# A two-layer graph attention kernel on one core: the order in which the score products take their operands, for every group of three half-blocks

## The chip, the core and the metric

The kernel runs on one core of a Trainium2 chip. The metric is the device time of one launch in microseconds (us), as the median of several runs; lower is better. TensorE (PE, with its weight loads shown as PEld), VectorE (DVE), ScalarE (ACT) and GpSimd (POOL) compute; SyncE (SP) issues most of the transfers. All data are fp32.

## What is computed

There are 128 graphs of 64 nodes with 768 features. The input is normalised, goes through two attention layers that share one adjacency matrix, and the result is added to the input. Cut to what matters:

```python
h = maximum(layernorm(x), 0)                      # x: 128 x 64 x 768
for l in range(2):
    m_left, m_right = h @ W_left[l].T, h @ W_right[l].T
    u_left  = einsum('bih,bjh->bij', h, m_left) / sqrt(768)
    u_right = einsum('bih,bjh->bij', h, m_right) / sqrt(768)
    u = u_left on and above the diagonal, u_right below it, where adj is set
    attention = exp(u) * adj, each row divided by its sum
    h = relu(layer_norm(attention @ (h @ W_lin[l].T)))
out = x + h
```

## The kernel before

Each layer has two passes. Pass one forms m_left and m_right for all tokens, multiplies them with h to scores, and turns these into attention weights that go to DRAM. Pass two forms h @ W_lin, applies the attention and normalises. The change touches pass one alone.

Pass one works on half-blocks of 256 tokens, called parts in what follows. There are 32: the first two form superblock 0, the other thirty form superblocks 1 to 10 of three parts each (`SUPER`, indexed by k). In a superblock, the multiplication by the two weight matrices, of 3 x 3 blocks each, is done by a fast scheme: `PRODUCTS` lists 40 products of a sum of weight blocks with a sum of token blocks, and `READS` says for each product to which of 18 outputs its running sum is added and with what factor. Output o belongs to part o // 6, to the left (0) or right (1) matrix by o // 3 % 2, and to the third o % 3 of the features; a third is two chunks of 128 features. So outputs 0 to 5 are part 0, 6 to 11 part 1, 12 to 17 part 2. The outputs of a part stand in one tile: in the listings of layer 0 `m_288` is part 0, `m_289` part 1 and `m_290` part 2.

The 40 products run one behind the other on PE, four matmuls of 128x256 each (two records each in the trace, so x8). They are spread over four running sums in four of six PSUM banks (C, D, X, Y, Z, V); product i goes on in the bank of i % 4, and the next superblock begins with the two other banks. `reads(i)` takes product i out of its bank: the first read into an output is a scaled copy on ACT (line 950), each later one an addition on DVE (lines 245 and 954). The next product in the same bank has to wait for that read.

An output is final with its last read. Product 39, the last of a superblock, is read into six outputs: 0, 4, 5 (part 0), 6, 7 (part 1) and 13 (part 2). All other outputs are final earlier.

The scores of superblock k - 1 are computed by `scores(k - 1)` while superblock k is already under way, behind the first four of its products (`SCORED = 3`), and before those four are read:

```python
if i == SCORED and k:
    scores(k - 1)
if i >= SCORED or k == 0:
    for n in waiting:
        reads(n)
```

So four products, some 7 us of PE, lie between the last product of a superblock and its scores. `scores` goes through 6 pairs of graphs q (two for each part) and 6 chunks c, and for each of these 36 units emits four matmuls of 32x95 (line 762, two records each: 288 for a superblock of three parts) that read the tile m of part q // 2 at chunk c and the part's tokens `ht`, and add up in the PSUM tile `sc`. The reads behind the scores overwrite m, so they wait for the units that read the same piece of m.

PE's order is that of the code, and so is DVE's and ACT's: the kernel writes it out by hand, with small jobs hung on numbered slots between the matmuls (`put`, `run`). Two orders exist. For the last superblock of each layer (`k == last`), the six reads of product 39 are sorted by `LAST_READ = (13, 6, 7, 0, 4, 5)` and the units of the scores by `SCORES_LAST`, a list of (part, chunks); for all other superblocks of three parts, reads go by output number and units by part, then pair, then chunk. There a pair's six chunks are one accumulation group of their own (`new` is set for its first chunk), and for the first and the last superblock one group spans all pairs in a bank.

Of the kernel before, what the change touches and what calls it, by code (L numbers as in the profile page):

```python
# [17 lines left out]
def kernel(  # L18
# [16 lines left out]
    C = H // P  # L35
# [31 lines left out]
    def put(slot, *fs):  # L67
        plan.setdefault(slot, []).extend(fs)

    def put_all(slot, fs, step=1):  # L70
        for f in fs:
            if f is not None:
                put(slot, f)
            slot += step
        return slot
# [5 lines left out]
    def run(slot):  # L81
# [30 lines left out]
    PRODUCTS = (  # L112
# [64 lines left out]
    def begins(k, l=0):  # L177
        return 0 if k == 0 else 2 * (len(PRODUCTS) if l else PLAIN) + 2 * len(PRODUCTS) * (k - 1)
# [65 lines left out]
    def added(eng, o, sign, a, b):  # L244
        (eng.tensor_add if sign == "+" else eng.tensor_sub)(o, a, b)  # L245
# [428 lines left out]
    def pass_one(l, start, final):  # L674
        with tc.tile_pool(name=f"one{l}", bufs=2, reuse_waits="tile") as sp, \
# [12 lines left out]
            def load_adj(k, queue=nc.sync):  # L688
                ADJ[k] = sp.tile([P, 6, 2, S], F32, name="adj", bufs=1)
                for u in sorted({p // 2 for p in SUPER[k]}):  # L690
                    at = [i for i, p in enumerate(SUPER[k]) if p // 2 == u]
                    q = [2 * (SUPER[k][i] % 2) for i in at]
                    for h in range(PAIR):
                        queue.dma_start(
                            ADJ[k][h * S:(h + 1) * S, 2 * at[0]:2 * at[-1] + 2].rearrange("p s k i -> p s (k i)"),
                            adj_t[u, h][:, q[0]:q[-1] + 2])
# [13 lines left out]
            def product(bank, w, ts, new, slot, n=TH):  # L710
                p = bank[:, :2 * n].rearrange("p (g n) -> p g n", g=2)
                for g in range(2):
                    for c in range(K2):
                        at = 0
                        for t in ts:
                            t = t[:, c]
                            n = math.prod(t.shape[1:])
                            o = p[:, g, at:at + n]
                            if len(t.shape) == 3:
                                o = o.rearrange("p (b s) -> p b s", b=t.shape[1])  # L720
                            nc.tensor.matmul(o, w[:, c, g * P:(g + 1) * P], t,  # L721
                                             start=(new and g == c == at == 0), stop=(c == K2 - 1),
                                             skip_group_check=True)
                            at += n
                    if g == 0:
                        turn_of(slot)

            def out_of(bank, thirds=False, o=0):
                if thirds:
                    p = bank[:, :4 * CUT].rearrange("p (g b s) -> p g b s", g=2, s=WIDE)  # L730
                    return p[:, :, :, THIRDS[o // 6][1]:]
                return bank.rearrange("p (g b s) -> p g b s", g=2, s=S)

            def into(o, thirds=False):
                v, k, i = o // 6, o // 3 % 2, o % 3
                if thirds:
                    r, n = THIRDS[v]
                    return both[:, i * K2:(i + 1) * K2, :, k, r + n:r + WIDE]
                return M[v][:, i * K2:(i + 1) * K2, :, k, :]

            def scores(k):
                nq = 2 * len(SUPER[k])
                p = KEEP["scores"].rearrange("p a (q m) -> p (a q) m", m=P)
                todo, begun, left = [(q, c) for q in range(nq) for c in range(C)], set(), {}
                if k == last:
                    todo.sort(key=lambda qc: next(n for n, (v, cs) in enumerate(SCORES_LAST)
                                                  if qc[0] // 2 == v and qc[1] in cs))
                if k == 0:

                    todo.sort(key=lambda qc: qc[1] < 3 if l else -(qc[0] // 2))  # L750
                for q, c in todo:
                    ht, m = HT[1, l, SUPER[k][q // 2]], M[q // 2]
                    left[q] = left.get(q, C) - 1
                    for h in range(PAIR):
                        b = q % 2 * PAIR + h
                        mb = both[:, c, q // 2 * PB + b] if l and k == 0 else m[:, c, b]
                        mb = mb.rearrange("p k j -> p (k j)")
                        for e in (0, 32):

                            new = (q // 4, h, e) not in begun if k in (0, last) else left[q] == C - 1  # L760
                            begun.add((q // 4, h, e))
                            nc.tensor.matmul(p[h * S + e:h * S + e + 32, q, e:e + 95],  # L762
                                             ht[:, c, b * S + e:b * S + e + 32], mb[:, e:e + 95],
                                             start=new, stop=not left[q], skip_group_check=k in (0, last))

            def chain(k):
                adj, nq = ADJ[k], 2 * len(SUPER[k])
# [42 lines left out]
            def softmax(k):  # L810
                CHAIN[k] = chain(k)
                return [lambda: next(CHAIN[k], None)] * 8
# [38 lines left out]
            def bank_of(n):  # L851
                n %= BANKS
                return KEEP["CD"][n] if n < 2 else KEEP["XYZV"[n - 2]]
# [79 lines left out]
            last = len(SUPER) - 1  # L933
            for k in range(FIRST_OF[l], len(SUPER)):
                assert slot == begins(k, l)
                if k:
                    put_all(slot + 2 * SCORED + 4, softmax(k - 1), 3)
                    put(slot + 2 * SCORED + 42, lambda k=k: load_adj(k, nc.sync if k == last else nc.scalar))
                if k == last:
                    final(slot, tokens)  # L940
                seen, waiting = set(), []

                def reads(i):
                    at_end = k == last and i == len(PRODUCTS) - 1
                    for o, c in sorted(READS[i], key=lambda oc: LAST_READ.index(oc[0])) if at_end else READS[i]:
                        bank = out_of(bank_of(CHAINS * (k - 1) + i % CHAINS), k == 0, o)
                        to = into(o, k == 0)
                        if o not in seen:
                            seen.add(o)
                            nc.scalar.activation(to, bank, AF.Copy, scale=float(c))  # L950
                        elif abs(c) == 1:
                            added(nc.vector, to, "+" if c > 0 else "-", to, bank)
                        else:
                            nc.vector.scalar_tensor_tensor(to, bank, float(c), to, op0=ALU.mult, op1=ALU.add)  # L954

                for i, (f, t) in enumerate(PRODUCTS):
                    while l and f not in weights.at:
                        fetch.popleft()()
                    w, tok = weights.need(f), tokens.need(k, t)
                    product(bank_of(CHAINS * (k - 1) + i % CHAINS), w, tok, i < CHAINS, slot, TH if k else 2 * CUT)  # L960
                    tokens.used(k, t)
                    if k == last:
                        weights.used(f)
                    waiting.append(i)
# [5 lines that stand above are left out]
                        waiting = []  # L970
                    turn_of(slot + 1)
                    slot += 2
# [5 lines left out]
            for i in (0, 1):  # L978
                LEAD[i] = fresh(l, i, (0, 1))
                multiply(l, 0, i, LEAD[i], (0, 1))  # L980
            scores(last)
            for f in steps[1:4]:
                f()
# [421 lines left out]
```

## Time and profile before

| | |
|---|---|
| runs | 2625.58, 2625.85, 2631.21 us |
| median | 2625.85 us |
| profiled execution | 2632.4 us, of which the span of the program is 2630.5 us |
| granted TensorE clock | 0.997 |
| busy share of the span | PE 98%, PEld 84%, DVE 67%, ACT 36%, POOL 67% |
| DMA | 331.83 MB, mean 126 GB/s |
| score matmuls (line 762) | 6144 records, 138.7 us busy on PE |

The profile is of one execution. Its 1.9 us beside the span are before the first and behind the last instruction. A row of the timeline gives the start and the length in us, the engine, the line, the operation, out<-in, how many instructions were merged into it, and in brackets the engine's idle time just before it with what ended that. Ends of matmuls are modelled, so the starts of the rows on PE are the safer reading. "issue" as the end of an idle time means that the engine waited for nothing that the profile shows.

### The profile page before, as it was taken

The numbers are of one execution on the slowest core, as the hardware profiler recorded it, in microseconds if no ns is written. First come the engines' busy times: TensorE is split into PE (matmuls) and PEld (weight loads), VectorE is DVE, ScalarE is ACT, GpSimd is POOL, SyncE is SP. The second block draws the span as 40 slices with busy tenths as digits, with TensorE's granted clock in tenths as the row PEclk, the third lists the DMA queues.
The fourth block names the chain that finished last, engine by engine and source line by source line (L and its number), as shares of the span: only waits on it lengthen the run. The fifth ranks groups of instructions, "written<-read, shape, count | busy, mean of one in ns | idle before, by whom it ended". The sixth has DMA issues, their size and how long they took to land.

```text
span 2630.5 us, 47267 instructions
## 1 busy us (share of the span) xinstructions
PE 2587.5 (98%) x18122; PEld 2214.9 (84%) x18122; DVE 1773.1 (67%) x2896; ACT 939.1 (36%) x1979; POOL 1756.7 (67%) x1384
## 2 busy tenths in 40 slices
PE   9899999999999999999999999999999999999998
PEld 8788888888888888888788888888888888788886
DVE  7878787777767445554457667677676666666667
ACT  5531213223113244444542222122222345555453
POOL 4766676666668657776267666667666668778776
PEclk9999999999999999999999999999999999999999
DMA  7534435333422354545795434253532215556555
GB/s 221 126 99 105 107 93 127 92 105 79 96 56 63 124 158 149 160 136 177 217 290 124 106 89 104 63 122 94 142 94 70 66 52 160 161 162 172 172 165 144
DMA packets 258464, 331.83 MB, mean 126 GB/s; under 512 B 56002, under 2 KB 190402, under 8 KB 258242
## 3 DMA queue, kind: packets, MB, share of 16 engines
q1 hardware_dynamic: 243106, 321.35, 44.1%
q10 hardware_dynamic: 15136, 7.48, 1.0%
q8 instruction: 145, 2.38, 0.4%
q14 instruction: 77, 0.63, 0.1%
HBM read 213.39 MB, written 115.34 MB: 125 GB/s over the span
## 4 chain that ended last, share of the span: by engine, by line
PE 89%; DVE 5%; ACT 3%; issue 1%; DMA 1%; SPq 0%; POOL 0%; DVEq 0%; ACTq 0%; POOLq 0%
PE Z L1047 13%; PE Y L721 9%; PE X L721 9%; PE C L721 9%; PE D L721 8%; PE Y L1047 8%; PE Z L721 8%; PE V L721 8%; PE X L1047 6%; PE sc L762 5%; PE V L1047 4%; PE aux L1089 2%; DVE m L245 2%; DVE st L352 1%; PE aux L1112 1%
## 5 line engine op out<-in xcount | busy, mean ns | idle before, releaser
L245 POOL TENSOR_TENSOR g<-ht 128x512 f32<-128x512 f32 (+1 forms) x608 | 777.5, 1290 | 404.0 <-ACT ht L395 84.0
L245 POOL TENSOR_TENSOR g<-g,g 128x512 f32<-128x512 f32 (+1 forms) x314 | 400.9, 1285 | 138.1 <-PE C L721 22.6
L245 POOL TENSOR_TENSOR g<-ht,g 128x512 f32<-128x512 f32 (+1 forms) x272 | 346.2, 1282 | 169.8 <-PE Z L721 44.6
L721 PE MATMUL X<-g,g 128*128 128x256 f32 (+1 forms) x1080 | 252.3, 376 | 0.4 <-DVE m L954 0.4
L1047 PE MATMUL Z<-g,g 128*128 128x256 f32 x1024 | 244.2, 380 | 1.1 <-ACT hl L316 0.8
L721 PE MATMUL C<-g,g 128*128 128x256 f32 x1008 | 239.3, 380 | 2.9 <-POOL g L245 2.9
L721 PE MATMUL Y<-g,g 128*128 128x256 f32 (+1 forms) x968 | 226.4, 377 | 7.5 <-POOL g L245 5.6
L721 PEld LDWEIGHTS X<-g,g 128*128 128x128 f32 x1080 | 202.5, 191 | 29.1 <-DVE m L954 1.1
L1047 PEld LDWEIGHTS Z<-g,g 128*128 128x128 f32 x1024 | 191.7, 190 | 33.2 <-issue 2.8
L395 ACT ACTIVATE ht<-ht,b_col,a_col 128x256 f32<-128x256 f32 x384 | 196.3, 592 | 58.9 <-DMA ht<-h 32.1
L721 PE MATMUL Z<-g,g 128*128 128x256 f32 (+1 forms) x936 | 217.0, 375 | 0.0
L721 PEld LDWEIGHTS C<-g,g 128*128 128x128 f32 x1008 | 190.4, 190 | 30.9 <-POOL g L245 4.1
L721 PE MATMUL D<-g,g 128*128 128x256 f32 x880 | 209.6, 381 | 2.3 <-POOL g L245 2.3
L721 PEld LDWEIGHTS Y<-g,g 128*128 128x128 f32 x968 | 182.2, 191 | 32.5 <-POOL g L245 8.9
L721 PE MATMUL V<-g,g 128*128 128x256 f32 (+1 forms) x840 | 193.7, 373 | 1.6 <-issue 1.6
L721 PEld LDWEIGHTS Z<-g,g 128*128 128x128 f32 x936 | 174.5, 190 | 23.0
L721 PEld LDWEIGHTS D<-g,g 128*128 128x128 f32 x880 | 168.2, 191 | 25.7 <-POOL g L245 2.7
L1047 PE MATMUL X<-g,g 128*128 128x256 f32 x768 | 182.5, 379 | 0.0
L721 PEld LDWEIGHTS V<-g,g 128*128 128x128 f32 x840 | 157.0, 190 | 21.6 <-issue 1.8
L1247 POOL TENSOR_TENSOR z<-z,b 128x768 f32<-128x768 f32 x62 | 112.7, 1830 | 82.0 <-DVE z L1244 77.5
L245 DVE TENSOR_TENSOR m<-m,Y 128x512 f32<-128x512 f32 (+2 forms) x196 | 126.4, 667 | 58.9 <-ACT m L950 35.3
L245 DVE TENSOR_TENSOR m<-m,D 128x512 f32<-128x512 f32 x180 | 118.2, 676 | 69.4 <-ACT m L950 51.4
(226 smaller groups left out, 4603.8 us busy)
## 6 DMA issues: line engine op xcount, KB each, us to landing
ht<-h SPq DMA_DIRECT2D x126, 768.0 KB, 6.0
h<-xb SPq DMA_DIRECT2D x124, 384.0 KB, 6.2
z<-z SPq DMA_DIRECT2D x128, 192.0 KB, 3.1
x<-z SPq DMA_DIRECT2D x128, 192.0 KB, 4.3
xr<-in_x_dram SPq DMA_DIRECT2D x120, 192.0 KB, 3.8
out_dram<-xr SPq DMA_DIRECT2D x120, 192.0 KB, 2.7
x<-in_x_dram SPq DMA_DIRECT2D x112, 192.0 KB, 4.7
g<-form SPq DMA_DIRECT2D x40, 256.0 KB, 4.9
```

Source lines behind the costliest of these rows:

```text
L245: (eng.tensor_add if sign == "+" else eng.tensor_sub)(o, a, b)
L352: nc.vector.bn_stats(st[:, n, :], halves[n])
L395: nc.scalar.activation(ht, ht, AF.Relu, bias=cols[1][:, c:c + 1], scale=cols[0][:, c:c + 1])
L721: nc.tensor.matmul(o, w[:, c, g * P:(g + 1) * P], t, start=(new and g == c == at == 0), stop=(c == K2 - 1), skip_group_check=True)
L762: nc.tensor.matmul(p[h * S + e:h * S + e + 32, q, e:e + 95], ht[:, c, b * S + e:b * S + e + 32], mb[:, e:e + 95], start=new, stop=not left ...
L1047: nc.tensor.matmul(p[:, n], b[t][:, c, r * P:(r + 1) * P], w[s][:, c, :], start=(i in FIRST and i not in PRELOAD and n == c == 0), stop=(c ...
L1089: nc.tensor.matmul(cx[k][i, m, :HH], at[j, q, :], hl[j, q, m * HH:(m + 1) * HH], start=True, stop=True)
L1112: nc.tensor.matmul(parts[r, k][n][i], at[j, q, :], hl[j, q, cut], start=True, stop=True)
L1247: nc.gpsimd.tensor_add(zs[k], zs[k], rows["b"])
```

## The change

The order that the last superblock had is given to every superblock but the first of each layer. The reads of product 39 now go 13, 6, 7, 0, 4, 5, and the score units go part 2 at chunks 0, 1, 4, 5; part 1 at chunks 4, 5; part 2 at chunks 2, 3; part 1 at chunks 0 to 3; part 0 at all chunks. The accumulation group spans all pairs of a bank everywhere. It concerns nine superblocks of each layer, 18 in all; the first and the last of each layer stay as they were.

```diff
                 todo, begun, left = [(q, c) for q in range(nq) for c in range(C)], set(), {}
-                if k == last:
+                if k:
                     todo.sort(key=lambda qc: next(n for n, (v, cs) in enumerate(SCORES_LAST)
                                                   if qc[0] // 2 == v and qc[1] in cs))
...
-                            new = (q // 4, h, e) not in begun if k in (0, last) else left[q] == C - 1
+                            new = (q // 4, h, e) not in begun
...
-                                             start=new, stop=not left[q], skip_group_check=k in (0, last))
+                                             start=new, stop=not left[q], skip_group_check=True)
...
-                    at_end = k == last and i == len(PRODUCTS) - 1
+                    at_end = k and i == len(PRODUCTS) - 1
```

The number of instructions stays the same on every engine, and on ACT, POOL and SP their order too. Two places change, both once in each of the 18 superblocks. The first is PE at the scores of superblock 2 in layer 0, between the products in banks Z and V and those in X and Y:

```order
 L721 MATMUL Z<-g_121,g_153 128x256 x4
 L721 MATMUL V<-g_152,g_142 128x256 x4
+L762 MATMUL sc<-m_290,ht 32x95 x32
+L762 MATMUL sc<-m_289,ht 32x95 x16
+L762 MATMUL sc<-m_290,ht 32x95 x16
+L762 MATMUL sc<-m_289,ht 32x95 x32
 L762 MATMUL sc<-m_288,ht 32x95 x48
-L762 MATMUL sc<-m_289,ht 32x95 x48
-L762 MATMUL sc<-m_290,ht 32x95 x48
 L721 MATMUL X<-g_129,g_150 128x256 x4
```

The 144 matmuls of part 0, 1 and 2 have become those of part 2, 1, 2, 1 and 0: part 0 has moved from the front to the end, and part 1 still ends after 96 of 144.

The second is DVE at the reads of product 39 (bank D) of the same superblock:

```order
 L422 SCALAR_TENSOR_TENSOR nb_1850<-mv_1847,rs_1849 128x4
+L245 TENSOR_TENSOR m_290<-m_290,D 128x8x64
+L245 TENSOR_TENSOR m_289<-m_289,D 128x8x64
+L954 SCALAR_TENSOR_TENSOR m_289<-D,m_289 128x8x64
 L245 TENSOR_TENSOR m_288<-m_288,D 128x8x64 x3
-L245 TENSOR_TENSOR m_289<-m_289,D 128x8x64
-L954 SCALAR_TENSOR_TENSOR m_289<-D,m_289 128x8x64
-L245 TENSOR_TENSOR m_290<-m_290,D 128x8x64
 L245 TENSOR_TENSOR m_289<-m_289,Y 128x8x64
```

The same six additions stand there; the three into part 0 have moved behind those into parts 2 and 1.

## The prediction

> **What bounds the kernel now.** I read the page first, for the engine that sets the time.
>
> ```profile
> span 2630.5 us, 47267 instructions
> PE 2587.5 (98%) x18122; PEld 2214.9 (84%) x18122; DVE 1773.1 (67%) x2896; ACT 939.1 (36%) x1979; POOL 1756.7 (67%) x1384
> PE 89%; DVE 5%; ACT 3%; issue 1%; DMA 1%; SPq 0%; POOL 0%; DVEq 0%; ACTq 0%; POOLq 0%
> ```
>
> PE is busy for 98% and holds 89% of the chain of waits, so a change that adds no work can win only PE's idle time. DVE's 5% of the chain is where to look. Next, the groups by line on PE for the score matmuls, and the view of that source line, which counts PE and PEld together.
>
> ```profile
> L762 PE MATMUL sc<-m,ht 128*32 128x95 f32 x6144 | 138.7, 246 | 9.7 <-issue 7.7 <-DVE m L245 1.2
> its engine sat idle before it (us, times) until:
>   issue: 26.2, 54
>   DVE m L245: 6.2, 16
> ```
>
> Line 762 waits for two things: DVE's additions into m, and "issue". The timeline of PE tells them apart. Here are an undisturbed superblock in the old order, one that waits for DVE, and the last superblock of layer 0, which has the new order already.
>
> ```profile
> 165.28 1.89 PE L721 MATMUL D<-g,g 128*128 128x256 f32 x8
> 167.10 4.60 PE L762 MATMUL sc<-m,ht 128*32 128x95 f32 x211
> 172.07 1.92 PE L762 MATMUL sc<-m,ht 128*32 128x95 f32 x77 [0.38 <-issue]
> 173.92 1.99 PE L721 MATMUL Z<-g,g 128*128 128x256 f32 x8
> ...
> 241.36 1.89 PE L721 MATMUL V<-g,g 128*128 128x256 f32 x8
> 243.55 7.04 PE L762 MATMUL sc<-m,ht 128*32 128x95 f32 x288 [0.30 <-DVE m L245]
> 250.52 1.99 PE L721 MATMUL X<-g,g 128*128 128x256 f32 x8
> ...
> 858.44 6.22 PE L762 MATMUL sc<-m,ht 128*32 128x95 f32 x288
> 864.59 1.78 PE L1047 MATMUL Z<-g,g 128*128 128x256 f32 x7
> ```
>
> Without a stop, 288 records take 864.59 - 858.44 = 6.15 us, 21.4 ns each. An "issue" gap comes in the middle of a batch (after record 211 here); a DVE wait comes at its start. The weight loads show that the second kind is three waits.
>
> ```profile
> 243.55 0.32 PEld L762 LDWEIGHTS sc<-m,ht 128*32 128x32 f32 x16 [0.70 <-DVE m L245]
> 244.14 0.32 PEld L762 LDWEIGHTS sc<-m,ht 128*32 128x32 f32 x16 [0.28 <-DVE m L245]
> 244.74 4.06 PEld L762 LDWEIGHTS sc<-m,ht 128*32 128x32 f32 x197 [0.28 <-DVE m L245]
> 249.09 1.28 PEld L762 LDWEIGHTS sc<-m,ht 128*32 128x32 f32 x59 [0.29 <-issue]
> ```
>
> Each 16 records are two chunks: PE stops for chunks 0, 2 and 4 of part 0, that is for outputs 0, 4 and 5, which DVE is just adding. One such batch has 0.30 on PE and 0.70 + 0.28 + 0.28 on PEld, 1.56 in all and four times. The 6.2 us and 16 times of the line are therefore four batches and nothing else, and so are PE's 1.2 us. The other 14 superblocks that the change touches wait for no addition. DVE's timeline shows why.
>
> ```profile
> 164.13 2.47 DVE L245 TENSOR_TENSOR m<-m,Y 128x512 f32<-128x512 f32 x4
> 166.52 0.68 DVE L954 SCALAR_TENSOR_TENSOR m<-Y,m 128x512 f32<-128x512 f32 x1
> 167.12 0.67 DVE L245 TENSOR_TENSOR m<-m,Y 128x512 f32<-128x512 f32 x1
> ...
> 242.82 2.46 DVE L245 TENSOR_TENSOR m<-m,D 128x512 f32<-128x512 f32 x4
> 245.21 0.67 DVE L954 SCALAR_TENSOR_TENSOR m<-D,m 128x512 f32<-128x512 f32 x1
> 245.81 0.67 DVE L245 TENSOR_TENSOR m<-m,D 128x512 f32<-128x512 f32 x1
> ```
>
> The six additions of product 39 take some 3.6 us at 0.6 each. In the first case they begin 3.0 us before the scores and stay ahead of them; in the second only 0.4 us before the place where the scores would begin.
>
> **The change part by part.** *The waits that go.* From D at 165.28 to the scores at 167.10 are 1.82 us, so the waiting batch should have begun at 241.36 + 1.82 = 243.18; it began at 243.55, 0.37 late. Sixteen records at 21.4 ns are 0.34 us, and the next two groups of loads came after 0.59 and 0.60, 0.25 late each. Together 0.87 us a batch, 3.5 us for four.
>
> *What is late next.* With the new order, DVE finishes output 13 at about 242.82 + 0.6 = 243.4, then 6, 7, 0, 4, 5 at 244.0, 244.7, 245.3, 245.9 and 246.5. PE needs 13 after 96 records (243.18 + 2.06 = 245.2), 6 after 128 (245.9), 0 after 192 (247.3), 4 after 208 (247.6) and 5 after 224 (248.0). The smallest slack is 1.5 us, so no addition is waited for, even in these four.
>
> *What is given back.* "issue" gaps stand 128 matmul records apart, as this batch, which has two of them, shows.
>
> ```profile
> 472.98 3.46 PE L762 MATMUL sc<-m,ht 128*32 128x95 f32 x156
> 476.72 2.82 PE L762 MATMUL sc<-m,ht 128*32 128x95 f32 x128 [0.28 <-issue]
> 480.18 0.36 PE L762 MATMUL sc<-m,ht 128*32 128x95 f32 x4 [0.63 <-issue]
> ...
> 395.96 6.28 PE L762 MATMUL sc<-m,ht 128*32 128x95 f32 x266 [0.30 <-DVE m L245]
> 403.09 0.69 PE L762 MATMUL sc<-m,ht 128*32 128x95 f32 x22 [0.85 <-issue]
> ```
>
> 128 matmuls with their weight loads are 256 instructions. [...] In the batch at 395.96 the gap after 266 puts earlier borders after 138 and 10; its waits after 16 and 32 records lie between those, and no gap is seen at 138. So 0.5 us of its 0.87 may come back there. [...] That leaves 3.5 - 0.5 = 3.0 us.
>
> [...]
>
> *The copies behind the scores.* The reads of the next superblock wait for the units that read m, and the next products for these reads.
>
> ```profile
> 170.97 1.08 ACT L950 ACTIVATE m<-Z 128x512 f32<-128x512 f32 x2 [15.25 <-PE sc L762]
> 171.94 1.09 ACT L950 ACTIVATE m<-V 128x512 f32<-128x512 f32 x2
> ...
> 174.05 2.06 ACT L950 ACTIVATE m<-D 128x512 f32<-128x512 f32 x4 [0.52 <-PE sc L762]
> ...
> 177.48 1.89 PE L721 MATMUL C<-g,g 128*128 128x256 f32 x8
> ```
>
> The first four copies go to part 1; output 10 was released after 22 of 36 units and is now after 24, 0.34 us later. Bank Z is free at 172.4 instead of 172.05 and its next product starts at 173.92: 1.5 us to spare. The copy into output 5 (bank C) read part 0, which was free early; now it waits for the end of the scores, starts at about 174.05, ends at 174.7, and PE wants the bank at 177.48. The four copies of bank D go to part 2, now released early, and follow behind it to about 176.8, before the product after that. No cost; it would be up to 1.2 us for each superblock if the release came only at the end of the scores.
>
> *At nothing:* the accumulation flags (the batch at 858.44 has them and ran without a stop), the sorting of six additions of one bank (the bank is free at the same time), and the instruction count, which does not change. On ACT, POOL and SP nothing moves.
>
> *Sum.* Against the profiled execution: 2632.4 - 3.0 = 2629.4 us. That execution was 6.5 us above the median of the runs, which holds two near 2625.7 and one at 2631.2. Carried to the median: 2625.85 - 3.0 = 2622.8 us.
>
> **The rivals.** [...]
>
> *The copies come late* (slower): if ACT were released only with the last unit, two copies of 1.08 us would end at 174.0 + 1.1 = 175.1 where PE goes on at 173.92, 1.2 us in each of 18 superblocks, 21.6 - 3.0 = 18.6 us net, 2644. It decides where the release slips by more than the 1.87 us between 172.05 and 173.92. Against it: ACT began at 170.97, well inside the scores, so release goes by pieces of m.
>
> *A hold-up at the end of layer 0.* These rows are an addition of means on DVE, PE's waits behind it, and the same place in layer 1.
>
> ```profile
> 823.50 4.13 DVE L229 TENSOR_SCALAR wmm<-wmm 128x2 f32<-128x2 f32 x1
> 828.36 1.97 PE L721 MATMUL Y<-g,g 128*128 128x256 f32 x8 [1.88 <-DVE m L245]
> 834.11 2.44 PE L721 MATMUL D<-ht,g 128*128 128x256 f32 x7 [2.05 <-DVE m L245]
> ...
> 2115.81 0.42 DVE L229 TENSOR_SCALAR wmm<-wmm 128x2 f32<-128x2 f32 x1
> 2122.72 1.99 PE L721 MATMUL D<-ht,g 128*128 128x256 f32 x8 [0.27 <-DVE m L245]
> ```
>
> A job of 0.42 us took 4.13, and PE lost 3.93 instead of 0.27 us: 3.7 us by how DVE and POOL happened to meet. If the two runs near 2625.7 lack it and 2631.2 has it, the median of the changed kernel may catch it: 2622.8 + 5.4 (the distance of those runs) = 2628.2. If it goes where it is now usual, the gain is 3.5 + 3.7 = 7.2 and the time 2618.7.
>
> [...]
>
> **How the numbers follow.** The waits go, 2622.8: 0.60. They move, 2625.4: 0.12. The hold-up comes in, 2628.2: 0.12. It goes too, 2618.7: 0.10. Late copies, 2644: 0.06. The range leaves out the last alone and allows about 1 us below and 2 us above for the scatter of a median: 2617.5 to 2630. A measurement of this kernel can tell about 0.2%, 5.3 us, from no change: below 2620.6 lie the 0.10 and, by scatter, 0.14 of the forecast's, 0.24; above 2631.1 the 0.06 and 0.02 of the hold-up's, 0.08; within, 0.68.
>
> **What would show it.** Right: "DVE m" is gone from the idle times of line 762, or below 0.5 us; the waiting batch at 243.55 shrinks from 9.16 us (241.36 to 250.52) to about 8.3; "issue" stays near 26 us; ACT's first copies begin about 0.3 us later after the scores' start, and no product of line 721 waits for ACT m. Wrong: new idle times before banks C, D or Z behind the scores, a sum for "issue" that grew by 3 us, or a total off by more than the hold-up explains.

## The result, and the profile after

The changed kernel ran in 2624.43 us (median of 20 runs, 2621.03 to 2631.0), the kernel before in 2629.44 (median of 20, 2625.58 to 2634.14). The ratio is 0.9982, with a 95% interval of 0.9976 to 0.9988: 4.7 us faster, 3.2 to 6.3 (the two medians lie 5.0 apart). Forecast were 2622.8 us and a gain of 3.0 us. The direction and the place were right; the gain was a little larger than the sum, and the three runs shown before were on the low side (2625.85).

The profiled execution after has a span of 2620.0 us, 10.5 less than that of before. Less than half of that is the change, as will be seen. The page and the view of line 762:

```profile
span 2620.0 us, 47281 instructions
PE 92%; ACT 3%; DVE 2%; DMA 2%; SPq 1%; issue 1%; POOL 0%; DVEq 0%; ACTq 0%; POOLq 0%
...
its engine sat idle before it (us, times) until:
  issue: 20.7, 51
  DVE st L352: 0.3, 1
```

The page counts 14 instructions more than before. They are semaphore waits on ACT (424 in place of 410), so the number of instructions is the same on every engine only for those that do work.

DVE's share of the chain fell from 5% to 2%, and "DVE m L245: 6.2, 16" is gone. The timeline of PE shows it in two of the four batches that waited:

```profile
241.83 1.89 PE L721 MATMUL V<-g,g 128*128 128x256 f32 x8
243.65 6.47 PE L762 MATMUL sc<-m,ht 128*32 128x95 f32 x288
250.06 1.13 PE L721 MATMUL X<-g,g 128*128 128x256 f32 x4
...
392.95 1.89 PE L721 MATMUL D<-g,g 128*128 128x256 f32 x8
394.77 5.74 PE L762 MATMUL sc<-m,ht 128*32 128x95 f32 x266
400.72 0.69 PE L762 MATMUL sc<-m,ht 128*32 128x95 f32 x22 [0.20 <-issue]
401.34 1.99 PE L721 MATMUL Z<-g,g 128*128 128x256 f32 x8
```

The scores follow the last product after 1.82 us, as in a batch that never waited. From the last product ahead to the first behind, the first batch takes 8.23 us in place of 9.16. DVE and ACT at the same place:

```profile
243.29 1.27 DVE L245 TENSOR_TENSOR m<-m,D 128x512 f32<-128x512 f32 x2
244.49 0.68 DVE L954 SCALAR_TENSOR_TENSOR m<-D,m 128x512 f32<-128x512 f32 x1
245.09 1.87 DVE L245 TENSOR_TENSOR m<-m,D 128x512 f32<-128x512 f32 x3
...
247.85 1.09 ACT L950 ACTIVATE m<-X 128x512 f32<-128x512 f32 x2 [0.60 <-PE sc L762]
248.82 1.09 ACT L950 ACTIVATE m<-Y 128x512 f32<-128x512 f32 x2
250.16 0.60 ACT L950 ACTIVATE m<-Z 128x512 f32<-128x512 f32 x1 [0.25 <-PE sc L762]
```

DVE is as late as it was: its additions begin 0.4 us before the scores and end at 246.96, but the last three are those into part 0, which PE now takes last. The first copy on ACT begins 4.2 us after the scores' start (3.9 in the undisturbed batch of before), and the copy into output 5 now waits for the end of the scores, 0.25 us, without PE noticing.

The rest of the 10.5 us is not the change. Below are the job on DVE that held up layer 0 before, at its place after, and its twin in layer 1:

```profile
818.62 0.46 DVE L229 TENSOR_SCALAR wmm<-wmm 128x2 f32<-128x2 f32 x1
2105.32 0.44 DVE L229 TENSOR_SCALAR wmm<-wmm 128x2 f32<-128x2 f32 x1
```

PE lost 0.26 us behind the first in place of 3.93. So some 3.7 us of the 10.5 are one hold-up that happened to be absent, 4.8 the four batches (37.93 to 33.11 us, below), and the other 2.0 are scatter in the 14 other batches: they took 119.7 us together in the first profile of before, 117.4 in its second and 117.4 after.

### The profile page after: what moved, and what is told of

Its sections match the earlier page's. It is cut to its first block, busy times and chain, and to the rows that moved or that the text cites. A ratio compares the mean times of both kernels' runs of the same rounds, so it can differ in the third digit from the quotient of the medians.

```text
span 2620.0 us, 47281 instructions
## 1 busy us (share of the span) xinstructions
PE 2584.0 (99%) x18122; PEld 2213.4 (84%) x18122; DVE 1769.9 (68%) x2896; ACT 939.7 (36%) x1979; POOL 1756.8 (67%) x1384
## 4 chain that ended last, share of the span: by engine, by line
PE 92%; ACT 3%; DVE 2%; DMA 2%; SPq 1%; issue 1%; POOL 0%; DVEq 0%; ACTq 0%; POOLq 0%
PE Z L1047 12%; PE Y L721 9%; PE X L721 9%; PE C L721 9%; PE D L721 9%; PE Z L721 8%; PE V L721 8%; PE Y L1047 8%; PE X L1047 6%; PE sc L762 5%; PE V L1047 4%; PE aux L1089 2%; PE aux L1112 1%; ACT g L237 1%; DVE g L538 1%
## 5 line engine op out<-in xcount | busy, mean ns | idle before, releaser
L245 POOL TENSOR_TENSOR g<-ht 128x512 f32<-128x512 f32 (+1 forms) x608 | 777.8, 1290 | 395.0 <-ACT ht L395 88.3
L245 POOL TENSOR_TENSOR g<-g,g 128x512 f32<-128x512 f32 (+1 forms) x314 | 401.1, 1285 | 137.0 <-PE C L721 21.4
L245 POOL TENSOR_TENSOR g<-ht,g 128x512 f32<-128x512 f32 (+1 forms) x272 | 346.3, 1282 | 169.4 <-PE Z L721 44.9
L1047 PEld LDWEIGHTS Z<-g,g 128*128 128x128 f32 x1024 | 191.7, 190 | 33.2 <-issue 2.8
L245 DVE TENSOR_TENSOR m<-m,Y 128x512 f32<-128x512 f32 (+2 forms) x196 | 126.5, 668 | 59.1 <-ACT m L950 35.2
L245 DVE TENSOR_TENSOR m<-m,D 128x512 f32<-128x512 f32 x180 | 118.2, 677 | 69.2 <-ACT m L950 45.3
```

The lines of the kernel that those rows point to most:

```text
L1047: nc.tensor.matmul(p[:, n], b[t][:, c, r * P:(r + 1) * P], w[s][:, c, :], start=(i in FIRST and i not in PRELOAD and n == c == 0), stop=(c ...
```

## The experiments

Two theories stood against each other. A: the gain is the waits of four batches in layer 0 (superblocks 2, 4, 6, 8), whose additions DVE finishes late. B: the new order shortens the issue gaps wherever it stands. C was that the hold-up makes the difference. The table sets the profiles side by side; "four batches" is the sum, over those four, of the time from the start of the last product ahead of the scores to the start of the first behind. The two columns of idle times add up PE and PEld as the view of line 762 does, so most stops are counted twice. They also hold an ordinary 0.33 us before the first weight load of each batch, which is no delay; it stands behind "issue" or, where an addition ended at about that time, behind DVE m.

| kernel | ratio to before, interval | four batches, us | idle at line 762 behind DVE m, us (times) | behind issue, us | hold-up of 4.1 us |
|---|---|---|---|---|---|
| before | 1 | 37.93 | 6.2 (16) | 26.2 | layer 0 |
| before again | 1.0001, 0.9993 to 1.0010 | 37.62 | 6.2 (16) | 21.1 | layer 1 |
| other fourteen | 1.0005, 0.9996 to 1.0013 | 37.86 | 6.2 (16) | 23.6 | none |
| after | 0.9982, 0.9976 to 0.9988 | 33.11 | 0 | 20.7 | none |
| after again | 0.9980, 0.9971 to 0.9989 | 33.36 | 0 | 23.0 | layer 1 |
| after beside the split | 0.9981, 0.9972 to 0.9990 | 32.90 | 0 | 22.7 | none |
| four only | 0.9981, 0.9973 to 0.9990 | 33.41 | 0 | 24.9 | none |
| scores alone | 0.9993, 0.9984 to 1.0002 | 37.14 | 10.4 (8) | 19.5 | none |
| reads alone | 1.0047, 1.0035 to 1.0059 | 46.37 | 29.0 (44) | 16.6 | none |
| statistics later | 0.9987, 0.9978 to 0.9996 | 33.50 | 0 | 22.2 | none |

**The four late superblocks only.** In both places that the change touches, `k` is replaced, and the accumulation groups follow the order of the units, here and in the next three kernels:

```diff
-if k:
+if k == last or (l == 0 and k in (2, 4, 6, 8)):
```

> The new order (reads of product 39 and score units) only in superblocks 2, 4, 6 and 8 of layer 0, those whose scores waited for an addition; the other 14 as before. Theory A (the gain is those four waits, 0.87 us each): 3.5 us faster than the kernel before, 2.5 to 5, ratio 0.9987, and no DVE m in the idle times of line 762. Rival B (the new order itself shortens the issue gaps wherever it stands: their sum fell from 26.2 to 20.7 us between the two profiles): only the part of four out of 18 superblocks of that, so about 3.5 + 0.3 us here and the rest of the 5 us in the other kernel. Rival C (the gain is the hold-up of 4.13 us at the end of layer 0, which the profile of after lacks): 0 to 5 us whatever the order, and the same in the kernel with the other 14.

Ratio 0.9981 (0.9973 to 0.9990): the whole gain, 5.0 us, at the upper end of what A allowed. The issue gaps did not fall with it (24.9 us).

**The other fourteen.** The condition is the other way round:

```diff
-if k:
+if k and not (l == 0 and k in (2, 4, 6, 8)):
```

> The new order in all superblocks of three parts except 2, 4, 6 and 8 of layer 0: the 14 whose scores waited for no addition. Theory A: no change, within 1 us, ratio 0.9997 to 1.0003, and the 16 idle times behind DVE m of 6.2 us stay. Rival B (issue gaps shorten under the new order): 1 to 4 us faster, ratio 0.9985 to 0.9996. Rival C: 0 to 5 us faster if the hold-up is gone, with the wait for DVE m at the end of layer 0 (1.88 + 2.05 us) gone from the profile.

Ratio 1.0005, interval 0.9996 to 1.0013: no gain, and the 6.2 us of waits stay. B falls: fourteen of eighteen reordered superblocks bring nothing that can be measured. The batch that stood at 395.96 keeps its waits here and has two gaps, of 0.21 us behind record 138 and of 0.63 behind record 266. The prediction saw none at 138 and took that for the work of the waits:

```profile
395.75 3.67 PE L762 MATMUL sc<-m,ht 128*32 128x95 f32 x138 [0.30 <-DVE m L245]
399.63 2.82 PE L762 MATMUL sc<-m,ht 128*32 128x95 f32 x128 [0.21 <-issue]
403.09 0.69 PE L762 MATMUL sc<-m,ht 128*32 128x95 f32 x22 [0.63 <-issue]
```

**The halves of the change.** First the order of the units with the old order of reads:

```diff
-at_end = k and i == len(PRODUCTS) - 1
+at_end = k == last and i == len(PRODUCTS) - 1
```

> The score units in the new order, the six reads of product 39 in the old one (0, 4, 5, 6, 7, 13). Theory A: output 13 is now the last of the six and is wanted after 96 of 288 records. In the four late batches it is ready at about 246.5 where PE wants it at 245.2 (times of the batch at 243.55), a wait of 1.3 us in place of 0.87: 0.7 to 1.7 us slower than before, ratio 1.0003 to 1.0006, and four waits for DVE m on PE after record 96, none in the other 14. Rival B: the order of the units alone makes it faster, 2 to 5 us, ratio 0.998 to 0.9992.

The waits came where expected. The timelines of PE and DVE at superblock 2:

```profile
243.24 2.17 PE L762 MATMUL sc<-m,ht 128*32 128x95 f32 x96
246.59 4.13 PE L762 MATMUL sc<-m,ht 128*32 128x95 f32 x192 [1.19 <-DVE m L245]
250.65 1.56 PE L721 MATMUL X<-g,g 128*128 128x256 f32 x6
...
245.87 0.67 DVE L245 TENSOR_TENSOR m<-m,D 128x512 f32<-128x512 f32 x1
```

After 96 records PE stops for the last addition, which ends at 246.54. From 243.24 + 2.06 = 245.30 to 246.59 that is 1.3 us, as forecast. But the ratio was 0.9993 (0.9984 to 1.0002) and not above 1: none of the four batches has an issue gap any more, and all take 9.2 to 9.5 us. In the five profiles without any of these waits the weight loads of the four stop for 1.1 to 1.7 us in mid-batch; here they don't, so a wait of 1.3 us in the middle goes with no gap later. I had counted on that for part of it only. The ratio can't be told from 1.

Then the order of the reads with the old order of units:

```diff
-if k:
+if k == last:
     todo.sort(...)
```

> The six reads of product 39 in the new order (13, 6, 7, 0, 4, 5), the score units in the old one. Theory A: output 0, which the scores want first, is now the fourth addition, ready at about 245.3 where the scores could begin at 243.2, then 0.25 us each for 4 and 5: about 2.7 us in each of the four late batches in place of 0.87, so 7 us slower than before, ratio 1.0028, 5 to 10 us; in the other 14 superblocks 0 to 0.1 us each. Rival B (the gain has nothing to do with the additions): no change, within 1 us.

```profile
241.97 1.89 PE L721 MATMUL V<-g,g 128*128 128x256 f32 x8
245.95 5.47 PE L762 MATMUL sc<-m,ht 128*32 128x95 f32 x229 [2.09 <-DVE m L245]
251.76 1.50 PE L762 MATMUL sc<-m,ht 128*32 128x95 f32 x59 [0.34 <-issue]
```

The scores begin at 245.95 in place of 241.97 + 1.82 = 243.79, 2.16 us late; with 0.25 each for outputs 4 and 5 that is the 2.7 us forecast. The total was worse than forecast, 1.0047 in place of 1.0028, and the loads of an undisturbed batch, superblock 1, show the reason:

```profile
167.60 0.66 PEld L762 LDWEIGHTS sc<-m,ht 128*32 128x32 f32 x32 [0.33 <-DVE m L245]
168.55 3.74 PEld L762 LDWEIGHTS sc<-m,ht 128*32 128x32 f32 x180 [0.28 <-DVE m L245]
```

After 32 records there is a wait of 0.28 us for output 5, and so it is in all 14: 3.9 us that I had put at 0 to 1.4. DVE's last addition ends 0.9 us behind the scores' start there, and output 5 is wanted after 0.7. With 4 x (2.66 - 0.87) = 7.2 us that makes 11.1 of the 12.4 measured. The four batches are in fact 8.6 us longer (46.37 against 37.8), so the rest lies in them, too. (The 0.33 us at the start is the ordinary one.) Neither half brought a gain that can be measured; the order of the additions and the order in which the scores take them must agree.

**The waits away without the new order.** The last test of A leaves both orders as they were, and takes away what makes DVE late: four row statistics that stand among the last reads of those superblocks. One number of the slots moves them behind the reads. Two of the four as they stand in the kernel before, and the additions of product 39 after the move:

```profile
234.23 1.01 DVE L352 BATCH_NORM_STATS2 st<-x 128x6 f32<-128x384 f32 x2
238.94 1.01 DVE L352 BATCH_NORM_STATS2 st<-x 128x6 f32<-128x384 f32 x2
...
243.04 2.48 DVE L245 TENSOR_TENSOR m<-m,D 128x512 f32<-128x512 f32 x4
```

```diff
-SPACE = (((0, 46, 97), (-12, 34, 97)), ...
+SPACE = (((0, 46, 97), (0, 34, 97)), ...
```

> The kernel before with its old order of reads and score units; only the preparation of every third block of rows in layer 0 (its four row statistics on DVE, 1.2 us each, which stand among the last reads of superblocks 2, 4, 6 and 8) begins 12 slots later, behind the reads of product 39. PE and POOL have the same instructions in the same order. Theory A (the gain is the four waits, whatever the order): the 16 idle times behind DVE m of 6.2 us go, the four batches shrink from about 9.4 to 8.3 us as in the changed kernel, 3.5 to 5 us faster than before, ratio 0.998 to 0.9987, unless the tokens of that block, ready some 10 us later, are now waited for by POOL and PE, which would show as idle time behind POOL g. A rival by which the order of units itself is the gain: no change, within 1 us.

```profile
244.20 1.89 PE L721 MATMUL V<-g,g 128*128 128x256 f32 x8
246.02 6.49 PE L762 MATMUL sc<-m,ht 128*32 128x95 f32 x288
252.44 1.78 PE L721 MATMUL X<-g,g 128*128 128x256 f32 x7
...
594.20 1.97 PE L721 MATMUL C<-g,g 128*128 128x256 f32 x8 [0.99 <-DVE m L954]
```

The additions begin 3.0 us before the scores at 246.02, as in an undisturbed superblock. In the old order the four batches now take 33.50 us, as in the new one, and nothing waits for DVE m at line 762. The ratio is 0.9987 (0.9978 to 0.9996). That it isn't 0.9982 may be scatter; but the price I had named shows, behind DVE and not behind POOL: PE waits 0.47, 0.62 and 0.99 us for DVE in the middle of three later superblocks (the last one is shown), and no other profile has these waits. The mechanism is the lateness of DVE; the order is one way of not meeting it.

**Both kernels again.**

> The kernel before, unchanged, against itself: shows what the measurement resolves (ratio 1.0000, within 0.0006) and, by its profile, which of the small stops come back. Theory A: the 16 idle times behind DVE m come back with 6.2 us, all in the four batches. Issue gaps of line 762: 20 to 27 us in sum if they are scatter, 26 if they belong to the old order. The hold-up of 4.13 us at 823.5 is there or not; A says nothing on it.

> The changed kernel once more on the chip of the others of this call: ratio 0.998 to 0.9988. No DVE m in the idle times of line 762. Issue gaps of line 762 between 20 and 27 us if they are scatter (theory A), 21 or below if the new order shortens them (rival B).

> The changed kernel on the same chip as the split one with the means on ACT, to compare those two: ratio to the kernel before 0.9975 to 0.9988. No DVE m in the idle times of line 762 and the four batches of layer 0 at 33 to 33.5 us in sum.

The kernel before against itself gives 1.0001, 0.9993 to 1.0010, which is what one such comparison resolves. The four batches came back within 0.3 us in each kernel, and the issue gaps at line 762 scatter from 21 to 26 us before and from 21 to 23 after. The hold-up came in layer 0 of the first profile of before, in layer 1 of the second and of one of after, and in neither layer of eight others: C falls, it comes with either kernel.

**The scores in two pieces.** The first 12 units read no output of product 39, so they can go behind product 1 of the next superblock (shortened):

```diff
+if i == EARLY and k > 1:              # EARLY = 1
+    scores(k - 1, 0)                  # units 0 to 11
 if i == SCORED and k:
-    scores(k - 1)
+    scores(k - 1, 1 if k > 1 else None)   # units 12 to 35
```

> The changed kernel, with the first 12 of the 36 score units (part 2 at chunks 0, 1, 4, 5 and part 1 at 4, 5: none of them reads an output of product 39) moved up behind product 1 of the next superblock; the other 24 stay behind product 3. [...] Expected: issue gaps of line 762 in the 20 superblocks fall to half or less, 3 to 6 us faster than the changed kernel, ratio to the kernel before 0.996 to 0.9975. [...] No new wait for DVE m or ACT m.

PE's timeline in superblock 2's products, and the same place in the changed kernel:

```profile
164.37 2.17 PE L765 MATMUL sc<-m,ht 128*32 128x95 f32 x96
166.47 1.99 PE L722 MATMUL C<-g,g 128*128 128x256 f32 x8
168.30 1.89 PE L722 MATMUL D<-g,g 128*128 128x256 f32 x8
170.12 4.13 PE L765 MATMUL sc<-m,ht 128*32 128x95 f32 x192
174.18 1.99 PE L722 MATMUL Z<-g,g 128*128 128x256 f32 x8
```

```profile
168.23 6.23 PE L762 MATMUL sc<-m,ht 128*32 128x95 f32 x288
174.39 1.99 PE L721 MATMUL Z<-g,g 128*128 128x256 f32 x8
176.22 1.89 PE L721 MATMUL V<-g,g 128*128 128x256 f32 x8
177.95 1.89 PE L721 MATMUL C<-g,g 128*128 128x256 f32 x8
```

Seven of the 18 superblocks kept a gap. If one adds up by how much records of PE follow each other later than 21.4 ns, where that is over 0.1 us, the gaps are 3.0 us together, where the changed kernel had 7.9 and 9.4 in its first two profiles. That is less than half, as expected; what makes a gap, and why two pieces have fewer, is not shown. The view's sum behind "issue" fell from 23.0 (after again) to 18.5 us only, but 0.33 us of it stand at the start of each piece, 21 times there and 35 times here; without them it is 16.1 and 6.9. (The view also has four idle times behind DVE m, 1.3 us: four such starts, none later than the others.) But the gain fell short of the 3 to 6 us expected: the ratio, 0.9975 (0.9966 to 0.9984), is only 1.3 us better than that of the changed kernel on the same chip, and the intervals overlap. The two pieces take 2.10 + 4.06 = 6.16 us, as the one did. A product behind scores, though, takes 1.83 us to the next start where others take 1.73, and scores begin 1.82 us after the product ahead of them: each extra change between the two costs 0.2 us, some 3.4 in all, more than half of the 4.9 to 6.4 won.

**The split with the column means on ACT.** In the split kernel:

```diff
-nc.vector.tensor_scalar_mul(mean, mean, -1.0 / H)
+nc.scalar.activation(mean, mean, AF.Copy, scale=-1.0 / H)
```

> The kernel with the score units in two pieces, and besides the scaling of the column means of the linear weights (128x2, three times in each layer) on ACT in place of DVE. In the nine profiles so far this job took 4.1 us in place of 0.44 in 3 of 18 places, and PE then lost 3.9 us in place of 0.26. If that hold-up belongs to the operation on DVE beside POOL, it cannot come back: 3.7 x 2 x 3/18 = 1.2 us faster than the split alone on average, ratio to the kernel before 0.9965 to 0.9975, and less scatter. If something else holds DVE up there, the same 4 us show in another instruction, and the ratio is that of the split alone, 0.9975.

> The split score units with the means on ACT again, beside the changed kernel: ratio to the kernel before 0.9955 to 0.997, 2 to 5 us faster than the changed kernel. If the first result was chance, the two are within 1 us of each other.

Ratios 0.9963 (0.9949 to 0.9976) and 0.9965 (0.9952 to 0.9977), the second beside the changed kernel's 0.9981: 2621.23 against 2625.12 us. It has the lowest medians of all kernels run, though the intervals still touch those of the changed kernel. What the job on ACT adds to the split alone (0.9975) isn't shown: those intervals overlap widely. Its two profiles have no hold-up; with 3 in 22 places elsewhere, that alone does not show that it can't come back.

## Why the prediction was right, and where it was off

- *Four batches and nothing else:* right. They alone give the whole gain, and the other fourteen none. The count of 16 waits and 6.2 us came back exactly in the two further profiles where the old order meets the late additions.
- *0.87 us a batch, 3.5 in all:* right for the waits themselves.
- *What is given back, 0.5 us:* the step that failed, in its sign. No run shows this term, nor that the waits move into the gaps (the 0.12 at 2625.4); both were estimates of mine. In the old order the four batches take 37.8 us (mean of three profiles, 37.62 to 37.93), in the new one 33.2 (four, 32.90 to 33.41): 4.6 us, 1.15 a batch. Besides the waits, their issue gaps shrank, by about 1 us together: the weight loads of the four stop behind "issue" in mid-batch for 2.2 to 2.5 us in the three profiles with the waits, for 1.1 to 1.7 in the five without. The batch at 395.96 had a gap of 0.85 us after record 266, at the same place after the change one of 0.20, and no gap came up at 138. In "other fourteen", where this batch keeps its waits, there was a gap of 0.21 us at 138, so the waits after 16 and 32 records don't always go with none there. "Statistics later" shows the same short batches in the old order, so it is the waits and not the order that go with longer gaps; why longer gaps go with waits at the start, while one wait after 96 records goes with none, no run here shows.
- *What is late next:* right; no addition is waited for, and the copies on ACT cost PE nothing.
- *"issue" near 26 us as a sign of being right:* it was no sign. The sum was 20.7 us after and 21.1 in the second profile of before; the gaps of 0.28 to 0.85 us that the prediction shows are some of a range from 0.16 to 1.20 in the same profile.
- *The hold-up:* right that it is apart from the change and of 3.7 us, but it does not account for the scatter of the runs, as the rival supposed: three hold-ups in 22 places make it rare, and the 20 runs of each kernel spread over 8.6 and 10.0 us. (The job is the scaling of the means, not an addition.)
- *The base:* 2622.8 rested on a median of three runs; on the median of 20 the same 3.0 us would have given 2626.4. That the forecast came within 1.6 us was luck: the base was 3.6 us too low, the gain 1.7 to 2 us too small, and the two errors partly cancel.

## What to carry over

When a long result is finished by several additions and then read at once, let the reader begin with what is final first and the writer finish first what is read first; only the two together brought anything here (ratio 0.9982), and one alone was slower (1.0047) or no better (0.9993). Moving other work out of the writer's way did much the same without any new order (0.9987). Before counting on such a change, count in the trace how many places really wait: 4 of 18 did here, and the other 14 gave nothing. And where two profiles differ by more than the change explains, profile both again before attributing the rest.

## What the runs showed of the hardware

The job of 128x2 on DVE that took 0.44 us in layer 1 after the change took 4.10 us at the same place when the changed kernel was profiled again. It stands here beside POOL's row of operations:

```profile
2105.78 4.10 DVE L229 TENSOR_SCALAR wmm<-wmm 128x2 f32<-128x2 f32 x1
...
2104.92 1.27 POOL L245 TENSOR_TENSOR g<-ht,g 128x512 f32<-128x512 f32 x1
2106.15 1.27 POOL L245 TENSOR_TENSOR g<-g,g 128x512 f32<-128x512 f32 x1
2107.37 2.49 POOL L245 TENSOR_TENSOR g<-ht 128x512 f32<-128x512 f32 x2
2111.76 1.28 POOL L245 TENSOR_TENSOR g<-g,g 128x512 f32<-128x512 f32 x1 [1.90 <-ACT g L237]
```

It ends at 2109.88, when POOL has run dry (2107.37 + 2.49 = 2109.86), three ends of POOL operations after that of the one beside which it began. In the other two hold-ups, too, it ends where POOL's row ends (827.63 and 827.60 in the first profile of before, 2114.85 and 2114.81 in its second). The case of 0.44 us after the change (2105.32) ends at 2105.76, where the POOL operation beside it does (2104.46 + 1.28 = 2105.74). That POOL held the job up is argued from these times and not shown, nor why it was for three operations more in 3 of 22 places. POOL itself then idled 1.90 us for a result of ACT (line 237) that hung on this job.
